# Sampling weights of a deformable convolution: products of mask and hat functions for three offsets in one instruction

## The chip, the core and the metric

The kernel runs on one core of a Trainium2 chip. Its time is the device time of one execution in microseconds (us). The core has five engines that run in parallel, each with its own queue of instructions in a fixed order: TensorE (matrix products; PE in the profile, and PEld for its weight loads), VectorE (DVE), ScalarE (ACT), GpSimd (POOL) and SyncE (SP, which here only starts transfers). An instruction that needs another engine's result, or a buffer that another engine still reads, waits at the head of its queue, and everything behind it waits too.

## The reference, cut to what matters

The kernel computes two layers over four images of 64x64 pixels and 256 channels: a deformable convolution, then an additive attention and a feed-forward layer on half of the tokens. The change lies in the first. There, for every pixel, 8 groups of channels are sampled at 9 points each. A small convolution of the normalised image gives, for each of the 72 points of a pixel, an offset in x, an offset in y and a logit; a softmax over the 9 points of a group makes the logits into masks:

```
offset = x1 @ off_w + off_b
mask = softmax((x1 @ mask_w + mask_b).reshape(N, H, W, G, 9))
out = sum over the points of  mask * bilinear(image, base position + offset)
```

The bilinear sample has four corners whose weights are products of a piecewise linear function (a "hat") of x and one of y.

## The kernel before, in words

The image is not gathered point by point. As long as an offset lies within one pixel, a sample falls on the 3x3 pixels around its base position, and the 9 points of a group together cover a 5x5 window. So the kernel works out, for every pixel and group, 25 weights, the tile `w5` (`w` in the profile), and then sums 25 shifted images times their weights. (Tokens with a larger offset are listed and recomputed by an exact gather of a few rows.)

The first stage is the generator `offsets_and_weights` (lines 267 to 607). It runs over 4 images and, for each, 8 slabs of 512 pixels: 32 turns, each with one "window". Pixels lie on the partitions: a slab is 4 rows of 128. Per turn:

- `taps` (line 492): TensorE makes `po`, the offsets and logits, from the convolution `x1`; VectorE adds the bias into `raw` and begins the softmax. The exponential is ScalarE's (line 513).
- `convolution` (line 462) of the next slab: 9 products per half of the channels on TensorE (`pc`), and a Silu on ScalarE (line 487). For the first image, half of it is made on VectorE (`x<-xn,dwk,x`).
- `window` (line 516): the softmax is finished; ScalarE makes the three hats of every offset, one for each of the pixel offsets -1, 0 and 1, in the tile `hat` [128, 3, 4, 144] (lines 528 to 530 and 533; the first 72 of 144 columns are x, the last 72 y). VectorE clears `w5` (line 537). Then, for each of three row offsets `ey`, `my` is mask times the y hat; for each of three column offsets `ex`, `mxy` is `my` times the x hat, and `mxy` is added to a 3x3 block of `w5` (lines 538 to 547). A product has 4 x 72 = 288 elements per partition.
- `projection` (line 427): TensorE projects the image (`pm`) and transposes it (`ptc`); ScalarE copies it to `tb` (line 456), which goes to memory as the table of the exact gather.
- `turn` (line 550): TensorE transposes `w5` of the turn before (`ptw`), ScalarE copies it, and it is stored to memory (`wt`).
- `front` of the next image: loads of x (`xt`, line 349, a pool `a_ld` with two buffers), transposes `pt`, statistics `st`, `mv`, `gv` on VectorE with two small products `pg` on TensorE, and normalisation.

Beside this stage runs the sampling of image 0 (`sample_image`): VectorE multiplies a shifted image with a loaded weight row (line 827, with `wb` loaded by SP) and adds it up (line 841), 400 instructions of 1024 elements. The main loop at lines 1528 to 1533 takes a fixed number of sampling steps at each `yield` of the stage.

The order on VectorE and on TensorE is that of the program for nearly all of these instructions (`vec` is `pinned`, `pe` is `Pinned`); a scheduler orders ScalarE, and SP's transfers. The stage starts with constants on SP's queue: `inw`, `inb`, `womr` and `wom` (weights of offsets and masks; the offset columns are reordered by VectorE, lines 288 to 292), `ombr`, `omb` (their bias), `dwk` and the normalisation's constants. Their pool `a_one` takes memory that a zero tile `zm` held until its stores to memory are done. What follows the stage (attention, feed-forward, sampling of images 1 to 3) does not use the changed lines.

Of the kernel before, what the change touches and what calls it, by code (L numbers as in the profile page):

```python
# [10 lines left out]
F32 = mybir.dt.float32  # L11
I32 = mybir.dt.int32
AF = mybir.ActivationFunctionType
ALU = mybir.AluOpType
# [3 lines left out]
P = 128  # L18
# [3 lines left out]
CC = C // P  # L22
G, K2 = 8, 9
GP = G * K2
# [22 lines left out]
def layers_kernel(ctx: ExitStack, tc: tile.TileContext, a, out: bass.AP):  # L47
    nc = tc.nc
# [19 lines left out]
    def load_const(pool, name, shape, src):  # L68
        t = pool.tile(shape, F32, name=name)
        nc.sync.dma_start(out=t, in_=src)  # L70
        return t
# [6 lines left out]
    def load_rows(pool, name, src):  # L78

        return load_const(pool, name, [P, src.shape[0]], src.partition_broadcast(P))  # L80
# [74 lines left out]
    with tc.tile_pool(name="selp", bufs=1) as sp, tc.tile_pool(name="ps_c", bufs=2, space=PSUM) as ps_c:  # L155
# [51 lines left out]
        out=below, in_=below, compare_op=ALU.is_gt, fill=0.0, base=0, pattern=[[1, P]], channel_multiplier=-1  # L207
# [27 lines left out]
    S = SimpleNamespace(bank=True, wants=False, gather=True, left=0, tables=[], listing=True)  # L235
# [31 lines left out]
    def offsets_and_weights(images, slab, rows_bufs):  # L267
# [5 lines left out]
        vec, pe = pinned, Pinned(nc.tensor)  # L273
        ca = S.a_one
# [6 lines left out]
        pb = S.a_t.tile([P, CC], F32, tag="pt", name="pb")  # L281
        nc.tensor.matmul(pb, permf, inb.rearrange("p k o -> p (k o)"), start=True, stop=True)
        nc.vector.tensor_copy(inbp, pb)
        womr = ca.tile([P, CC, 2 * GP], F32, name="womr")
        nc.sync.dma_start(out=womr, in_=a["L0_conv_off_w"].rearrange("(k p) f -> p k f", p=P))
        wom = ca.tile([P, CC, 3 * GP], F32, name="wom")
        nc.sync.dma_start(out=wom[:, :, 2 * GP :], in_=a["L0_conv_mask_w"].rearrange("(k p) f -> p k f", p=P))
        for k in range(CC):
# [1 line left out]
                wom[:, k, : 2 * GP].rearrange("p (o s) -> p o s", o=2),  # L290
                womr[:, k].rearrange("p (s o) -> p o s", o=2),
            )
        ombr = load_rows(ca, "ombr", a["L0_conv_off_b"])
        omb = ca.tile([P, 1, 3 * GP], F32, name="omb")
        nc.sync.dma_start(out=omb[:, 0, 2 * GP :], in_=a["L0_conv_mask_b"].partition_broadcast(P))
        nc.vector.tensor_copy(
# [18 lines left out]
        for base, sign in ((0, 1), (7, -1)):  # L315
            nc.gpsimd.affine_select(
                out=gavg, in_=gavg, compare_op=ALU.is_ge, fill=0.0, base=base,
# [101 lines left out]
        def image(at):  # L419
# [96 lines left out]
            def window(s):  # L516
                raw, m3, red, rbc = raws.pop(s)
                vec.tensor_reduce(red, m3, AX.X, ALU.add)
                vec.reciprocal(red, red)
                vec.tensor_tensor(m3, m3, rbc, ALU.mult)  # L520
                nc.sync.dma_start(
                    out=raw_d[n][s * slab * P : (s + 1) * slab * P].rearrange("(t p) j -> p t j", p=P), in_=raw
                )


                off = raw[:, :, : 2 * GP]
                hat = S.a_w1p.tile([P, 3, slab, 2 * GP], F32, tag="hat", name="hat")
                nc.scalar.activation(hat[:, 0], off, AF.Relu, scale=-1.0)
                nc.scalar.activation(hat[:, 2], off, AF.Relu)
                nc.scalar.activation(hat[:, 1], off, AF.Abs)  # L530
                vec.tensor_reduce(omax[:, n, s * slab : (s + 1) * slab], hat[:, 1], AX.X, ALU.max)
                yield
                nc.scalar.activation(hat[:, 1], hat[:, 1], AF.Identity, scale=-1.0, bias=one_c)

                w5 = S.a_wk.tile([P, slab * G, WIN, WIN], F32, tag="w5", name="w5")
                w5s[s] = w5
                vec.memset(w5, 0.0)
                for ey in range(3):
                    my = S.a_w1p.tile([P, slab, GP], F32, tag="my", name="my")
                    vec.tensor_mul(my, raw[:, :, 2 * GP :], hat[:, ey, :, GP:])  # L540
                    for ex in range(3):
                        mxy = S.a_w1p.tile([P, slab, GP], F32, tag="mxy", name="mxy")
                        vec.tensor_mul(mxy, my, hat[:, ex, :, :GP])
                        blk = w5[:, :, ex : ex + 3, ey : ey + 3]
                        vec.tensor_tensor(
                            blk, blk, mxy.rearrange("p t (g i j) -> p (t g) i j", i=3, j=3), ALU.add
                        )
                    yield

            def turn(s):  # L550
# [12 lines left out]

            return SimpleNamespace(
                projection=projection, convolution=convolution, taps=taps, window=window, turn=turn
            )

# [940 lines left out]
    with scope(("one", 1, 0)):  # L1508
        zm = S.one.tile([P, 2 * G * 2 * CG], F32, name="zm")
        nc.gpsimd.memset(zm, 0.0)  # L1510
        for n in range(NB):
            tabw = tab_d[n].rearrange("(q g) c -> q (g c)", g=G)
            for q0 in (0, (H + 2) * MP):
                for f in range(CC):
                    nc.scalar.dma_start(out=xp_d[n][f][:, q0 : q0 + 2 * MP], in_=zm[:, : 2 * MP])
                nc.scalar.dma_start(
                    out=tabw[q0 : q0 + 2 * MP].rearrange("(p r) c -> p (r c)", r=2), in_=zm[:MP]
# [3 lines left out]
    with scope(  # L1521
        ("a_one", 1, 0), ("a_xn", 2, 0), ("a_ld", 2, 0), ("a_wk", 2, 0), ("a_w1p", 1, 0), ("a_sm", 2, 0),
        ("smp", 2, 0), ("two", 2, 0), ("sb", 2, 0), ("dn", 1, 0), ("a_t", 3, 1), ("a_m", 3, 1), ("ps_m", 2, 1),
    ):
        slabs = NT * 2 // SLAB
        S.listing = S.gather = False
        first = sample_image(0, 2)
        for at, i in enumerate(offsets_and_weights(range(NB), SLAB // 2, 1)):
            if i == slabs + 1:
                S.listing = S.gather = True  # L1530

            for _ in range((3, 3, 2, 2, 2)[at % 5] if i < slabs else (4, 4, 3, 3, 3)[at % 5]):
                next(first, None)
        for _ in first:
            pass
# [76 lines left out]
```

## Time and profile before

| | us |
|---|---|
| median of 3 runs | 10418.23 (10410.31 to 10430.02) |
| profiled execution, own time | 10422.25 |
| its span, first to last instruction | 10420.5 |
| first add to `w5` / last add to `w5` (start) | 131.6 / 1341.5 |
| `my` products, 96 of 128x288, mean | 0.458 |
| `mxy` products, 288 of 128x288, mean | 0.458 |
| adds to `w5`, 288 of 128x288, mean | 0.465 |
| TensorE clock granted, mean (1 is full speed) | 0.933 |

The profile is one execution, recorded by the hardware. It has the busy time of each engine, groups of equal instructions with their mean duration, the idle time of the engine just before them, and what ended that idle time. Where a group's idle time is large and the engine is the one that sets the pace, that is where to look; on another engine it costs nothing. Most instructions of this stage carry the line number 263, that of a helper which keeps program order, so that they are told apart by their tiles.

### The profile page before, as it was taken

The page shows a single profiled execution, that of the slowest core. Times are in us where ns is not written, and L with a number is a line of the kernel's source. Part 1 is how long each engine was busy: PE and PEld are TensorE (multiplying, and loading weights), DVE is VectorE, ACT ScalarE, POOL GpSimd, SP SyncE. Part 2 cuts the span into 40 slices and gives each one's busy share as a digit, 9 for nine tenths or more (in the row PEclk, how much of TensorE's full clock was granted, in tenths as well). Part 3 has the DMA queues.
Part 4 walks back from the last instruction along what each step waited for, and adds up shares of the span by engine and source line. Part 5 has one row for each costly group of instructions (what it writes and reads, how often), then busy time and mean ns, then how long its engine had stood idle before and what let it go on. Part 6 is the DMA issues. An engine that isn't in the chain of part 4 may idle for free. (4 is left out here: it accounts for less than half of the span.)

```text
span 10420.5 us, 117367 instructions
## 1 busy us (share of the span) xinstructions
PE 9281.3 (89%) x38892; PEld 4511.9 (43%) x38892; DVE 8523.7 (82%) x13743; ACT 7466.9 (72%) x8526; POOL 5246.2 (50%) x3058
## 2 busy tenths in 40 slices
PE   5777779999999589999999589999999699999995
PEld 3444434444444344444444344444444344444443
DVE  5888879898989579899898679899898367777772
ACT  3333358888888348888888248888887389999991
POOL 0131037775555237676655247676555255555552
PEclk8888879999999689999999689999999799999997
DMA  3565532221222341112111442122111300000002
GB/s 107 179 201 181 179 119 64 64 65 61 72 66 67 129 144 54 51 55 54 53 58 44 144 131 54 53 52 55 53 59 37 103 13 8 10 7 7 7 5 76
DMA packets 375450, 766.10 MB, mean 74 GB/s; under 512 B 49360, under 2 KB 204656, under 8 KB 374800
## 3 DMA queue, kind: packets, MB, share of 16 engines
q1 hardware_dynamic: 282000, 600.32, 17.8%
q0 software_dynamic: 32448, 54.39, 3.2%
q10 hardware_dynamic: 60352, 103.50, 2.8%
q8 instruction: 313, 5.13, 0.2%
q14 instruction: 337, 2.76, 0.1%
HBM read 580.88 MB, written 177.14 MB: 73 GB/s over the span
## 5 line engine op out<-in xcount | busy, mean ns | idle before, releaser
L1035 DVE TENSOR_TENSOR r<-nn,r 128x512 f32<-128x512 f32 x6144 | 3946.0, 684 | 853.7 <-PE nn L1030 793.9
L1030 PE MATMUL nn<-qn,kf 32*128 32x512 f32 (+1 forms) x12288 | 4521.5, 641 | 131.4 <-DVE r L1035 95.2
L1120 POOL TENSOR_TENSOR r<-r 128x1024 f32<-128x1024 f32 x1024 | 2708.6, 2645 | 2656.6 <-DVE r L1035 2613.8
L1114 ACT ACTIVATE r<-d 128x1024 f32<-128x1024 f32 x3072 | 3113.7, 1014 | 1083.5 <-DVE r L1124 705.4
L1020 PE MATMUL d<-qf,kf 32*128 32x512 f32 (+1 forms) x12288 | 3337.6, 632 | 75.3 <-ACT r L1114 74.1
L1116 ACT ACTIVATE r<-r 128x1024 f32<-128x1024 f32 x3072 | 3124.9, 1051 | 32.7
L1030 PEld LDWEIGHTS nn<-qn,kf 32*128 32x128 f32 (+1 forms) x12288 | 1401.4, 185 | 1900.4 <-DVE r L1035 1450.5
L1058 PE MATMUL pv<-v,et 128*128 128x257 f32 x8192 | 2100.0, 399 | 14.5 <-DVE acv L1082 14.5
L1058 PEld LDWEIGHTS pv<-v,et 128*128 128x128 f32 x8192 | 1504.3, 193 | 972.5 <-issue 767.5
L1020 PEld LDWEIGHTS d<-qf,kf 32*128 32x128 f32 (+1 forms) x12288 | 1018.4, 186 | 1339.4 <-issue 690.1
L1122 POOL TENSOR_TENSOR r<-r 128x512 f32<-128x512 f32 x1024 | 1333.4, 1302 | 93.7 <-DVE r L1035 18.0
L827 DVE TENSOR_TENSOR prd<-xs,wb 128x1024 f32<-128x1024 f32 x768 | 979.6, 1275 | 36.1 <-DMA wb<-wt 30.1
L841 DVE TENSOR_TENSOR ac<-ac,prd 128x1024 f32<-128x1024 f32 x768 | 997.3, 1299 | 6.3
L722 POOL DMA_INDIRECT ga<-tab,tii x576 | 698.6, 1213 | 329.4 <-DVE so L736 174.2
L1042 ACT ACTIVATE et<-et,nshift 128x512 f32<-128x512 f32 x1024 | 723.8, 707 | 31.0 <-DVE et L1127 31.0
L1124 DVE TENSOR_TENSOR r<-r 128x512 f32<-128x512 f32 x1024 | 722.8, 706 | 4.1 <-POOL r L1120 3.7
L1127 DVE TENSOR_TENSOR et<-r 128x512 f32<-128x512 f32 x1024 | 699.9, 684 | 0.4
L263 PE MATMUL pc<-xn,diag 128*128 128x512 f32 x1008 | 447.1, 600 | 14.5 <-ACT xn L397 8.3
L263 PE MATMUL ptc<-ident,xp 128*128 128x128 f32 (+1 forms) x576 | 140.3, 359 | 213.9 <-ACT tb L456 212.7
L787 POOL TENSOR_TENSOR xr<-xr,outb 128x512 f32<-128x512 f32 x64 | 90.4, 1419 | 473.6 <-DMA xr<-in_x_dram 416.6
L263 PEld LDWEIGHTS pc<-xn,diag 128*128 128x128 f32 x1008 | 190.9, 192 | 246.1 <-issue 223.0
L1426 POOL DMA_INDIRECT sort<-v,rif x128 | 133.2, 1040 | 291.6 <-DVE rif L263 176.2
(343 smaller groups left out, 5249.2 us busy)
## 6 DMA issues: line engine op xcount, KB each, us to landing
wb<-wt SPq DMA_DIRECT2D x800, 512.0 KB
tab<-tb ACTq DMA_DIRECT2D x128, 256.0 KB
v<-t SPq DMA_DIRECT2D x64, 512.0 KB
xs<-xp SPq DMA_DIRECT2D x32, 680.0 KB
xp<-xp ACTq DMA_DIRECT2D x32, 544.0 KB
xt<-in_x_dram SPq DMA_DIRECT2D x32, 512.0 KB
xr<-in_x_dram SPq DMA_DIRECT2D x64, 256.0 KB
t<-xr SPq DMA_DIRECT2D x64, 256.0 KB
```

The source lines that it names most:

```text
L263: return lambda *args, **kw: keep(op(*args, **kw))
L827: keep(nc.vector.tensor_tensor(pr.rearrange("p (r w) -> p r w", w=W), src, wb.rearrange("p (r w) -> p r w", w=W), ALU.mult,))
L841: keep(nc.vector.tensor_add(ac[:, f, :], ac[:, f, :], pr))
L1020: keep(nc.tensor.matmul(d[:, j, :], kf[g, blk, rows(kt)], qs[q][0][g, blk, :], start=True, stop=True))
L1030: keep(nc.tensor.matmul(nn, kf[g, blk, rows(kt)], qs[q][1][g, blk, :], start=True, stop=True))
L1035: keep(nc.vector.tensor_tensor(r[:, j, :], ns[j], r[:, j, :], ALU.mult))
L1042: keep(nc.scalar.activation(ets[b], ets[b], AF.Exp, bias=nshift))
L1058: keep(nc.tensor.matmul(pv, ets[b0 + i][:, rows(j)], v[:, k0 + i, :], start=(i == 0), stop=(i == PVB - 1)))
L1114: keep(nc.scalar.activation(rs[b, p], ds.pop((b, p)), AF.Ln))
L1116: keep(nc.scalar.activation(rs[b, p], rs[b, p], AF.Exp, scale=-1.0))
L1120: keep(nc.gpsimd.tensor_tensor(rs[b, 1], rs[b, 1], rs[b, 2], ALU.add))
L1122: keep(nc.gpsimd.tensor_tensor(rs[b, 1][:, 0], rs[b, 1][:, 0], rs[b, 3][:, 0], ALU.add))
```

## The change

In `window`, the mask is multiplied with the y hats of all three offsets by one instruction, in place in `hat` (864 elements), and for each `ey` the three x hats are multiplied by one instruction into a tile `mxy` three times as large. The operand that is the same for the three offsets (the mask, or `my` of one `ey`) is read three times, with a stride of zero. The adds to `w5` are as before. A window has 1 + 3 products of 864 elements and 9 adds, where it had 3 + 9 products of 288 and 9 adds.

The larger `mxy` takes memory. To make room, the tiles `womr` and `ombr`, used once at the start, are no longer in the pool of constants: they take the two buffers of the pool `a_ld` that the loads of x (`xt`) use afterwards.

```diff
-        womr = ca.tile([P, CC, 2 * GP], F32, name="womr")
+        womr = S.a_ld.tile([P, CC, 2 * GP], F32, tag="xt", name="womr")
         nc.sync.dma_start(out=womr, in_=a["L0_conv_off_w"].rearrange("(k p) f -> p k f", p=P))
...
-        ombr = load_rows(ca, "ombr", a["L0_conv_off_b"])
+        ombr = S.a_ld.tile([P, 2 * GP], F32, tag="xt", name="ombr")
+        nc.sync.dma_start(out=ombr, in_=a["L0_conv_off_b"].partition_broadcast(P))
...
                 vec.memset(w5, 0.0)
+                mask = raw[:, :, 2 * GP :].rearrange("p t (o k) -> p o t k", o=1).to_broadcast([P, 3, slab, GP])
+                my = hat[:, :, :, GP:]
+                vec.tensor_tensor(my, mask, my, ALU.mult)
                 for ey in range(3):
-                    my = S.a_w1p.tile([P, slab, GP], F32, tag="my", name="my")
-                    vec.tensor_mul(my, raw[:, :, 2 * GP :], hat[:, ey, :, GP:])
+                    mxy = S.a_w1p.tile([P, 3, slab, GP], F32, tag="mxy", name="mxy")
+                    vec.tensor_tensor(
+                        mxy, my[:, ey : ey + 1].to_broadcast([P, 3, slab, GP]), hat[:, :, :, :GP], ALU.mult
+                    )
                     for ex in range(3):
-                        mxy = S.a_w1p.tile([P, slab, GP], F32, tag="mxy", name="mxy")
-                        vec.tensor_mul(mxy, my, hat[:, ex, :, :GP])
                         blk = w5[:, :, ex : ex + 3, ey : ey + 3]
                         vec.tensor_tensor(
-                            blk, blk, mxy.rearrange("p t (g i j) -> p (t g) i j", i=3, j=3), ALU.add
+                            blk, blk, mxy[:, ex].rearrange("p t (g i j) -> p (t g) i j", i=3, j=3), ALU.add
                         )
                     yield
```

## The prediction

> **What bounds the kernel now.** I read the page from the top: engine totals, then the 40 slices, to find what the changed lines overlap with.
>
> ```profile
> PE 9281.3 (89%) x38892; PEld 4511.9 (43%) x38892; DVE 8523.7 (82%) x13743; ACT 7466.9 (72%) x8526; POOL 5246.2 (50%) x3058
> PE   5777779999999589999999589999999699999995
> DVE  5888879898989579899898679899898367777772
> PEclk8888879999999689999999689999999799999997
> ```
>
> A slice is 260.5 us. In the first five TensorE is busy 50 to 70%, VectorE 80%; after that comes attention, with TensorE at 90%. The changed lines run only in the first stage, `offsets_and_weights`, so I asked for the busy time of its later stretches (columns: stretch, length, busy time and count of PE, PEld, DVE, ACT, POOL, then clock, DMA share, GB/s).
>
> ```profile
> 570.00:840.00 270.00, 213.42 (x656) 122.49 (x657) 243.44 (x345) 100.26 (x165) 104.05 (x102) 0.82 0.71 207
> 840.00:1276.00 436.00, 327.53 (x1005) 187.99 (x1004) 388.03 (x537) 150.35 (x248) 34.14 (x26) 0.85 0.57 185
> 1276.00:1345.00 69.00, 51.26 (x172) 33.35 (x172) 30.65 (x64) 24.03 (x43) 3.65 (x4) 0.80 0.29 99
> ```
>
> VectorE is 90% busy from 570 to 1276 us, TensorE 75 to 79%, and from 1276 VectorE only 44%. So VectorE looks like the limit, but not everywhere. What it does there, from the groups of VectorE between 130 and 1345 us (busy, mean ns | idle before, releaser):
>
> ```profile
> L841 DVE TENSOR_TENSOR ac<-ac,prd 128x1024 f32<-128x1024 f32 x192 | 237.5, 1237 | 4.0
> L263 DVE TENSOR_TENSOR w<-w,mxy 128x288 f32<-128x288 f32 x288 | 134.0, 465 | 9.5
> L263 DVE TENSOR_TENSOR mxy<-my,hat 128x288 f32<-128x288 f32 x288 | 131.9, 458 | 12.8 <-ACT hat L533 1.4
> L263 DVE TENSOR_TENSOR my<-raw,hat 128x288 f32<-128x288 f32 x96 | 43.9, 458 | 0.0
> L263 DVE SCALAR_TENSOR_TENSOR x<-xn,dwk,x 128x512 f32<-128x512 f32 x48 | 36.0, 749 | 1.6
> L263 DVE TENSOR_TENSOR raw<-po,omb 128x432 f32<-128x432 f32 x62 | 35.7, 602 | 63.0 <-PE po L263 63.0
> ```
>
> The products to be merged take 131.9 + 43.9 = 175.8 us. The last row is the warning: VectorE waits 63.0 us in this stage for TensorE's `po`. Then what TensorE waits for, same stretch (total, times, longest):
>
> ```profile
> PE ptc L263 <- ACT tb L456: 212.7, 169, 6.4
> PE pmo L783 <- DVE ac L841: 16.5, 4, 12.8
> PE pg L263 <- DVE mv L263: 13.7, 2, 8.9
> PE pg L263 <- DVE gv L263: 10.0, 2, 5.1
> PE pt L263 <- DVE st L263: 9.1, 3, 6.1
> ```
>
> TensorE's large wait is for the copies `tb` on ScalarE, a loop that VectorE has little part in (each `tb` waits for the next `ptc`, or for the store `tab<-tb`). Its waits for VectorE come to some 60 us. So two chains run side by side, of nearly one length: VectorE's, and TensorE with ScalarE.
>
> Last, a window in order of time on VectorE (start, length):
>
> ```profile
> 1255.34 0.72 DVE L263 MEMSET w<- 128x800 f32 x1
> 1255.98 0.40 DVE L263 TENSOR_TENSOR my<-raw,hat 128x288 f32<-128x288 f32 x1
> 1256.41 0.46 DVE L263 TENSOR_TENSOR mxy<-my,hat 128x288 f32<-128x288 f32 x1
> 1256.91 0.46 DVE L263 TENSOR_TENSOR w<-w,mxy 128x288 f32<-128x288 f32 x1
> 1257.47 0.46 DVE L263 TENSOR_TENSOR mxy<-my,hat 128x288 f32<-128x288 f32 x1
> 1257.96 0.46 DVE L263 TENSOR_TENSOR w<-w,mxy 128x288 f32<-128x288 f32 x1
> ```
>
> Dependent instructions start 0.49 us apart. One row offset (my, three mxy, three adds) takes 3.34 us, here from 1255.98 to 1259.32, a window 10.0 us.
>
> **What the Trainium skill says.** "VectorE: DVE Perf Modes", section on the TRN2 errata, gives an fp32 `tensor_tensor` as (N + 151)/0.96 ns and attributes a fixed cost to every instruction. The trace agrees: 457 ns computed for 288 elements against 458 measured, 1224 for 1024 against 1237. "Perfetto Trace Analysis", section Optimization Strategy, says to find the gaps on the engine that limits a regime and what each of them waits for; the 63.0 us above is such a gap, and it shows that VectorE does not limit the whole stage. Neither page prices a broadcast operand in a three-level pattern; the trace shows one, `ga<-ga,wg` 128x1152 at 1352 ns, where the formula gives 1357. So I price the new products, of 864 elements, at (864 + 151)/0.96 = 1057 ns.
>
> **The change, part by part.**
> (1) Products. A window loses 3 + 9 products of 458 ns, 5.50 us, and gains 1 + 3 of 1057 ns, 4.23 us: 1.27 us of busy time. Eight instructions fewer also save eight gaps of about 0.03 us between end and dependent start (0.49 against 0.458): together 1.5 us. 32 windows (4 images, 8 slabs): 48 us of VectorE, if every one counted. The adds into w5 stay, 9 a window.
> (2) All three hats are now needed at the first product, which had needed one. The middle hat (ScalarE, line 533) ended 1.9 us or more ahead of the first product in windows 4 to 27. In 28 it ended 2.8 us after it, of which 1.4 was waited already; in 0 and 2 it ended 0.6 after it. Cost 2.6 us in all, in windows whose gain is lost anyway (below).
> (3) `womr` and `ombr` take the two buffers of `xt`. The first two loads of x, issued at 2.16 us before, now stand on SP's queue behind the constants, the first of which is issued at 61.99 because the zeroing stores hold its memory. With two issues fewer ahead of them they go at about 66.5 and 67.0; a load of x takes some 4 us until its transposes start (the fourth chunk's buffer came free at about 75, its transposes started at 79.04), so the first transposes move from 65.45 to about 70.6. That is covered: the fourth transpose group waited until 74.08 for VectorE's statistics, which wait for `diag`, and `dwk` now arrives two issues (1 us) earlier. Loads 2 to 7 follow one buffer's cycle of 5.9 us and end within 0.5 us of where they did. The megabyte taken from the first microseconds can bring `outw` earlier, for which VectorE idled 1.46 us at 10.37. Taken as zero; ends a gain of 1.5 and a loss of one cycle, 5.9.
> (4) Order. Compiled, every engine has the same instructions after this stage. Within it ScalarE has line 530 ahead of a Silu in some ten windows (0.67 us each way), and the listing of tokens (windows 7 and 8) moves on VectorE and TensorE. VectorE waited 10.3 us for the listing's `pl`; bounds 10 us either way, taken as zero.
>
> **How much arrives.** I keep a lead for each chain. VectorE's grows 1.5 us a window. TensorE's can grow only where it waited for VectorE, by no more than that wait. Where VectorE waited for TensorE, its lead falls back to TensorE's. From the rows in order of time: windows 0 to 4 each run into a wait for `po` (6.2, 1.7, 10.3, 1.8, 4.4 us): lead 0.9 at 282 us, from the 1.2 TensorE waited at 141. 5 to 7 gain, but TensorE, waiting 1.7 through line 533 at 364, takes 1.7 of it: 2.6, and 8 to 10 are lost to waits on `pl` and `po` (3.5 at 517). Window 11, then TensorE waits 8.9 for `mv` at 570: 4.1. 12 lost. 13 and 14, `pmo` waits 2.7 at 663: 6.6. 15 to 17, TensorE waits 1.0 at 757 and 1.9 at 795: 9.5. 18 lost (4.6 at 839). 19 and 20, TensorE waits 1.6 at 916: 11.1. 21 to 23, 0.7 at 1051: 11.8; then VectorE waits 4.4 at 1095 for ScalarE. 25 to 28 stay level, since VectorE waits 0.7, 1.4 and 1.6 for ScalarE there. 29 ends in the 12.8 us wait of `pmo` at 1276: 13.3. 30 lost (7.5 at 1324), and the last window counts whole, as the last `ptw` waited 5.2 us for it: 14.8. So 15 of 48 us. The profiled execution took 10422.25 (span 10420.5 and 1.75 around it): 10407 on its own scale. The median of the runs, 10418.23, lies 4.0 lower: 10403.
>
> **The rivals.**
> Nearly all arrives: VectorE sets the pace throughout, 24 to 48 us, so 10394 to 10370. For: 90% busy against 75 to 79%. Against: the `po` waits, and that TensorE with its `tb` waits is as full.
> Hidden: TensorE and ScalarE set the pace, and their waits for VectorE were slack. Then only the last window counts, less a load cycle: 10423 to 10412. Against: the 12.8 us at 1276.
> Slower: the repeated operand, whose outer stride is zero, does not stream at one element per cycle. At half rate a product takes 1958 ns and a window 2.1 us more; ten windows have waits that absorb it, 22 do not: 46 us, 10464. It decides from 1057 + 1500/4 = 1432 ns on. Against: `ga<-ga,wg`.
> The change does do what it says: the compiled order has 128 products for 384.
>
> **How the numbers follow.** The three runs before span 20 us, so 0.2%, 21 us, is about what can be told from no change. Partial arrival (6 to 21 us) 0.50; nearly all (over 21) 0.28; hidden or a slight loss 0.13; slower by over 21 us 0.09. With a little of the first passing the bound: faster 0.29, same 0.62, slower 0.09. The range goes to 10376 (42 us arrive) and to 10428 (the hidden case with a load cycle lost and the runs' scatter); the likeliest case alone has 10397 to 10412.
>
> **What would show it.** Products of 128x864 at 1.06 us, 128 of them; a window's VectorE work at 8.5 us; waits for `po` longer than 63.0 us in total, as VectorE arrives earlier; the first stage's last w5 add at about 1327 instead of 1341.5; everything later shifted unchanged. Wrong: products over 1.4 us; the last add at 1300; or the first transposes after 75 us.

## The result, and the profile after

The changed kernel took 10401.21 us (median of 11 runs, 10395.03 to 10422.86), the kernel before 10423.14 in the same session (11 runs, 10410.31 to 10434.86): a ratio of 0.9981, with a 95% interval of 0.9972 to 0.9989. That is about 20 us less, 11 to 29. The forecast was 10403, or 15 us less. The profiled execution took 10410.61 us with a span of 10408.9 (before 10422.25 and 10420.5).

The page of the changed kernel, engine totals and two rows of the 40 slices:

```profile
PE 9286.8 (89%) x38892; PEld 4522.6 (43%) x38892; DVE 8493.1 (82%) x13487; ACT 7467.8 (72%) x8526; POOL 5252.1 (50%) x3058
...
PE   5778789999999589999999589999999699999995
...
DVE  6888879898989679899898679899898367777772
```

VectorE has 256 instructions fewer (8 in each of 32 windows) and 30.6 us less of busy time; the slices look nearly as before. The stretches of the first stage (columns as in the prediction: busy time and count of PE, PEld, DVE, ACT, POOL, then clock, DMA share, GB/s):

```profile
570.00:840.00 270.00, 212.38 (x664) 124.27 (x665) 231.75 (x288) 101.65 (x166) 96.90 (x94) 0.82 0.69 201
840.00:1276.00 436.00, 344.87 (x1053) 200.14 (x1052) 369.68 (x445) 151.04 (x248) 35.81 (x28) 0.85 0.56 185
1276.00:1345.00 69.00, 36.38 (x156) 29.53 (x154) 43.94 (x136) 18.48 (x36) 1.85 (x2) 0.62 0.49 170
```

Between 840 and 1276 us VectorE's busy time falls from 388.03 to 369.68 us and TensorE's rises from 327.53 to 344.87: TensorE gets through more of its work in the same time. The last stretch is no longer the same work, since the stage now ends in its middle. VectorE's groups between 130 and 1345 us (busy, mean ns | idle before, releaser):

```profile
L263 DVE TENSOR_TENSOR w<-w,mxy 128x288 f32<-128x288 f32 x288 | 133.3, 463 | 9.3
L263 DVE TENSOR_TENSOR mxy<-hat 128x864 f32<-128x864 f32 x96 | 101.2, 1054 | 1.4
L263 DVE TENSOR_TENSOR raw<-po,omb 128x432 f32<-128x432 f32 x62 | 36.0, 602 | 75.0 <-PE po L263 74.8
...
L263 DVE TENSOR_TENSOR hat<-raw,hat 128x864 f32<-128x864 f32 x32 | 32.5, 1017 | 1.3 <-ACT hat L534 1.1
```

The products take 101.2 + 32.5 = 133.7 us, where they took 175.8. From its first product to its last add, other instructions in between included, a window takes 15.8 us (median of 32), where it took 17.4; the 32 sum to 479.7 us for 526.8. VectorE's wait for `po` has grown from 63.0 to 74.8 us. What TensorE waits for in the same stretch (total, times, longest):

```profile
PE ptc L263 <- ACT tb L457: 199.8, 167, 6.5
PE pmo L787 <- DVE ac L845: 14.6, 3, 10.2
```

These were 212.7 and 16.5. The last window in order of time on VectorE (start, length; x3 is three instructions drawn as one row):

```profile
1301.10 0.72 DVE L263 MEMSET w<- 128x800 f32 x1
1301.92 1.06 DVE L263 TENSOR_TENSOR hat<-raw,hat 128x864 f32<-128x864 f32 x1
1303.01 1.06 DVE L263 TENSOR_TENSOR mxy<-hat 128x864 f32<-128x864 f32 x1
1304.10 1.45 DVE L263 TENSOR_TENSOR w<-w,mxy 128x288 f32<-128x288 f32 x3
1305.58 1.06 DVE L263 TENSOR_TENSOR mxy<-hat 128x864 f32<-128x864 f32 x1
```

The last add into `w5` ends at 1310.7 us, where it ended at 1342.0: 31.3 us earlier. So more was gained in the stage than the 20 us of the whole, and that had to be explained.

### The profile page after: what moved, and what is told of

Its sections match the earlier page's. It is cut to its first block, busy times and chain, and to the rows that moved or that the text cites. A ratio compares the mean times of both kernels' runs of the same rounds, so it can differ in the third digit from the quotient of the medians.

```text
span 10408.9 us, 117078 instructions
## 1 busy us (share of the span) xinstructions
PE 9286.8 (89%) x38892; PEld 4522.6 (43%) x38892; DVE 8493.1 (82%) x13487; ACT 7467.8 (72%) x8526; POOL 5252.1 (50%) x3058
## 5 line engine op out<-in xcount | busy, mean ns | idle before, releaser
L1062 PE MATMUL pv<-v,et 128*128 128x257 f32 x8192 | 2106.5, 401 | 14.8 <-DVE acv L1086 14.8
L1126 POOL TENSOR_TENSOR r<-r 128x512 f32<-128x512 f32 x1024 | 1333.7, 1302 | 100.1 <-DVE r L1039 24.4
```

What stands on the lines that cost most here:

```text
L1062: keep(nc.tensor.matmul(pv, ets[b0 + i][:, rows(j)], v[:, k0 + i, :], start=(i == 0), stop=(i == PVB - 1)))
L1126: keep(nc.gpsimd.tensor_tensor(rs[b, 1][:, 0], rs[b, 1][:, 0], rs[b, 3][:, 0], ALU.add))
```

## The experiments

All kernels ran on the chip beside the kernel before. "Last add" is the end of the last add into `w5` in the profiled execution; "preparation" is the time there between the first and the eighth `mm<-pq,bqk` of VectorE, which are the first and last units of the first attention preparation. The ratio is to the kernel before on the same chip. "Three buffers" is explained with its run.

| kernel | last add, us | preparation, us | ratio, 95% interval |
|---|---|---|---|
| before | 1342.0 | 53.8 | 1 |
| constants moved, products as before | 1332.0 | 62.9 | 1.0003 (0.9994 to 1.0012) |
| changed | 1310.7 | 62.9 | 0.9981 (0.9972 to 0.9989) |
| changed, again | 1317.7 | 56.8 | 0.9975 (0.9963 to 0.9986) |
| changed, matmuls after the stage | 1312.2 | 55.2 | 0.9978 (0.9968 to 0.9988) |
| changed, mxy made twice | 1374.3 | 54.1 | 1.0031 (1.0019 to 1.0042) |
| changed, three adds fewer | 1308.4 | 53.7 | 0.9962 (0.9948 to 0.9977) |
| changed, more copies to tb | 1339.8 | 53.6 | 1.0003 (0.9994 to 1.0012) |
| before, three buffers | 1307.4 | 58.1 | 0.9963 (0.9951 to 0.9976) |
| before, three buffers, again | 1305.6 | 63.0 | 0.9969 (0.9957 to 0.9981) |
| changed, three buffers | 1269.8 | 62.9 | 0.9943 (0.9927 to 0.9960) |
| changed, three buffers, again | 1274.2 | 58.0 | 0.9944 (0.9931 to 0.9957) |
| changed, three buffers, matmuls after the stage | 1282.8 | 63.5 | 0.9951 (0.9937 to 0.9965) |
| changed, three buffers, three adds fewer | 1258.7 | 53.9 | 0.9926 (0.9912 to 0.9940) |

**The changed kernel again.** No edit.

> The changed kernel once more, to see what repeats. Theory A (the clock): the last w5 add again within 3 us of 1310.2, and between 1395 and 1420 us some 9 of the 31 us are given back again, because TensorE stays at half clock until about 1402. Theory B (scatter): the last add or the end of the preparation lies more than 5 us elsewhere, so that the 31 and the 9 say nothing. Time: 10401, ratio 0.998.

Time 10412.75 us against 10442.63 on this chip, ratio 0.9975: the gain is there again, 26 us (15 to 39). But the last add came at 1317.7, 7 us later than in the first profile, and the preparation took 56.8 us, not 62.9. So theory B holds for the details: neither the 31 us nor the giving back of 9 us repeats as it stood. One profile tells the end of this stage to some 7 us (13 us between three executions of one and the same stage with three buffers: 1269.8, 1274.2, 1282.8); the ratios tell more.

**Where the 31 us were gained.** I set the two traces side by side, matmul by matmul, up to the last add. The lead is the start in the kernel before minus the start in the other; each step of it above 0.25 us is put down to the tile at which it appears. Before against changed: `ptc` 10.5, `pmo` 4.7, `ptw` 3.9, `pt` 2.5, `pso` 1.8, `pg` 1.4, the start 2.3, the rest 4.2. The five tiles for which TensorE waited on VectorE (`pmo`, `ptw`, `pt`, `pso`, `pg`) make 14.3 us. Against the second execution of the changed kernel they make 11.4, but there `ptc`, which waits for ScalarE's copies `tb`, makes only 0.9. In its place 9.4 us come at the `po` products, in steps below 0.25 us. These are no waits: the records of `po` start 247 ns apart on average in that execution, for 267 in the kernel before and 263 in the first execution, and fewer of the 512 fall into stretches of half clock (176, for 231 and 220). Between the two executions of the changed kernel, that is with nothing changed at all, `ptc` moves by 8.5 us and `po` by 7.7.

The kernel that has only the constants moved (its run is told below) serves as a second "before": its last add comes at 1332.0. Measured from it, the lead at the last add is 21.3 and 14.3 us; the five tiles make 12.7 and 9.9 of it, `ptc` 8.6 and 0.3. So the part of the five tiles repeats, at 10 to 14 us, and that of `ptc` does not. One place where `ptc` moves is around 1070 us. TensorE there in the kernel before:

```profile
1076.30 0.69 PE L263 MATMUL ptc<-ident,xp 128*128 128x128 f32 x2 [4.67 <-ACT tb L456]
```

The same row in the changed kernel:

```profile
1058.97 0.69 PE L263 MATMUL ptc<-ident,xp 128*128 128x128 f32 x2 [0.86 <-ACT tb L457]
```

And in the kernel that has only the constants moved and makes the products as before:

```profile
1067.01 0.69 PE L263 MATMUL ptc<-ident,xp 128*128 128x128 f32 x2 [0.86 <-ACT tb L457]
```

A wait of 4.67 us becomes one of 0.86 in both, so these 3.8 us are not the products' doing. Behind the 4.67 us ScalarE's copy waits 4.27 us for the store `tab<-tb` that still reads the buffer; in the kernel with only the constants moved the copy at this place waits 0.45 us for it.

**Only the constants moved.** The kernel before, with this part of the diff alone:

```
-        womr = ca.tile([P, CC, 2 * GP], F32, name="womr")
+        womr = S.a_ld.tile([P, CC, 2 * GP], F32, tag="xt", name="womr")
...
-        ombr = load_rows(ca, "ombr", a["L0_conv_off_b"])
+        ombr = S.a_ld.tile([P, 2 * GP], F32, tag="xt", name="ombr")
+        nc.sync.dma_start(out=ombr, in_=a["L0_conv_off_b"].partition_broadcast(P))
```

> The kernel before with womr and ombr moved into the buffers of xt, and nothing else: the products stay twelve. The prediction took this part for nothing: first window at 128.5 to 130.5 for 130.0, last w5 add 1337 to 1345, ratio 0.9995 to 1.0005. Were it part of the gain, the last add would come at 1330 to 1336 and the ratio be near 0.999.

10427.62 us against 10428.63, ratio 1.0003. The first window starts at 129.8 us for 130.0. The last add at 1332.0 would fit the other theory, but the ratio does not: the interval leaves the part a gain of at most 0.06%, of the 0.22% in the whole. Most of the gain, then, is the products', and all of it as far as this run can tell.

**The products made twice.** In the changed kernel:

```
                     mxy = S.a_w1p.tile([P, 3, slab, GP], F32, tag="mxy", name="mxy")
-                    vec.tensor_tensor(
-                        mxy, my[:, ey : ey + 1].to_broadcast([P, 3, slab, GP]), hat[:, :, :, :GP], ALU.mult
-                    )
+                    for _ in range(2):
+                        vec.tensor_tensor(
+                            mxy, my[:, ey : ey + 1].to_broadcast([P, 3, slab, GP]), hat[:, :, :, :GP], ALU.mult
+                        )
```

> Each mxy product is made twice, 1.09 us more each, 3.27 us a window, 105 us of VectorE in 32 windows; the result is the same. If VectorE sets the pace of the stage nearly everywhere, the last w5 add moves from 1310 to 1405-1415 (slope 0.9 to 1). If two chains of one length share it, as the prediction had it (15 of 48), the slope upward still nears 1, since TensorE's chain is then left behind: 1390-1415. If TensorE with ScalarE set the pace and VectorE had slack, below 1370. The whole: plus 60 to 100 us.

59 us more than the changed kernel on the same chip (10471.88 against 10412.75), and a last add 60 us later than the mean of its two profiles (1374.3 against 1314.2): 0.56 of the 105 us. That fits none of the three theories: VectorE does not set the pace nearly everywhere (0.9 to 1), and is not slack (below 1370). Upward too, about half arrives.

**Three adds fewer.**

```
-                    for ex in range(3):
+                    for ex in range(3) if ey != 1 else ():
```

> Leaves out the three adds into w5 of the middle row offset, so the sums lack them: 3 x 0.48 = 1.46 us a window, 47 us of VectorE in 32 windows. If VectorE still sets the pace as it did for the change (31 of 48), the last w5 add comes at about 1280 (slope 0.65). If the TensorE chain is now the limit, as the prediction's leads said, 1295 to 1310 (slope below 0.3), with waits for po far above 75 us.

10398.72 against 10412.75 us: 14 us of 47, with intervals that overlap. (The kernel leaves out three adds in nine, so its weights are incomplete.) The last add, at 1308.4, is 2 to 9 us earlier. VectorE's wait for `po` rises to 89.4 us. This fits the second theory: after the change, VectorE has little left to give.

**More work on ScalarE.** In the changed kernel, each second copy to `tb` is made twice:

```
                         nc.scalar.copy(tb[:m, :, :, c, :], pt[:m, c].rearrange("p f (e g) -> p f g e", g=GH))
+                        if c:
+                            nc.scalar.copy(tb[:m, :, :, c, :], pt[:m, c].rearrange("p f (e g) -> p f g e", g=GH))
```

> The changed kernel with every second copy tb<-ptc made twice on ScalarE: 144 more at 0.39 us, 56 us of ScalarE in the stage, result the same. If the chain of TensorE and ScalarE has no slack after the change, the last w5 add comes 40 to 56 us later, at 1355 to 1370. If its waits are slack behind VectorE, 5 to 20 us later: 1318 to 1335.

The ratio is 1.0003 where the changed kernel has 0.9978 (the mean of 0.9981 and 0.9975): 26 us. The last add moves from 1314.2 to 1339.8, also 26: 0.46 of 56 us. Between the two theories again. VectorE's wait for `po` is now 98.0 us.

**A third buffer for the copies.** In the changed kernel, and the same in the kernel before; `inw` is used up before the first copy, so its 2 KB per partition make the room:

```
-        inw = load_const(ca, "inw", [P, CC, C], a["L0_conv_in_w"].rearrange("(k p) f -> p k f", p=P))
+        inw = S.a_ld.tile([P, CC, C], F32, tag="tb", name="inw", bufs=3)
+        nc.sync.dma_start(out=inw, in_=a["L0_conv_in_w"].rearrange("(k p) f -> p k f", p=P))
...
-                    tb = S.a_ld.tile([P, CC, GH, 2, CG], F32, tag="tb", name="tb")
+                    tb = S.a_ld.tile([P, CC, GH, 2, CG], F32, tag="tb", name="tb", bufs=3)
```

> The changed kernel with a third buffer for tb (inw is loaded into one of them to make room), so that ScalarE's copies wait less for the stores tab<-tb (92 to 99 us in the stage). Theory two chains: after the change TensorE with ScalarE sets the pace, so the stage gains a good part of that: last w5 add at 1285 to 1300, time 10 to 25 us below the changed kernel's. Theory VectorE sets the pace: last add 1308 to 1320, as it was, and ScalarE's wait only moves to another row.

> The kernel before with the same third buffer for tb. If before the change VectorE set the pace, the buffer is worth clearly less here than in the changed kernel: last w5 add 1333 to 1342, ratio 0.9990 to 1.0005. If the two chains wait for each other at many places, it is worth about the same in both: last add 1315 to 1330, ratio 0.998.

The changed kernel takes 10369.19 us, ratio 0.9943; the kernel before 10389.58, ratio 0.9963. ScalarE's wait for the stores, in the changed kernel's stage:

```profile
ACT tb L457 <- DMA tab<-tb: 91.9, 46, 5.9
```

and in the changed kernel with three buffers:

```profile
ACT tb L458 <- DMA tab<-tb: 36.0, 17, 4.2
```

Some 58 us less of waiting (means 95.4 and 37.8 over two profiles each) bring 36 us in the changed kernel and 35 in the kernel before (0.9978 to 0.9943, and 1 to 0.9966). That is more than any theory had expected: the last adds, at 1269.8 and 1307.4, lie ahead of all the ranges. The moved `inw` isn't what brings it, since the first add into `w5` comes at about the same time (133.1 us in the changed kernel for 132.3, 131.3 in the kernel before for 131.6). That it brings about the same in both speaks for the theory of chains that wait for each other at many places, and against the one in which VectorE set the pace before and TensorE after.

**Both again,** to see whether the third buffer lets more of the products' gain arrive:

> The changed kernel with three tb buffers, once more: last w5 add within 8 us of 1269.8, ratio 0.994, the fastest version so far.

> The kernel before with three tb buffers, once more. With the run above it gives what the merged products are worth where no copy waits for a store: if ScalarE's waits for stores were what kept part of the 48 us back, the two last w5 adds lie 33 to 45 us apart (two buffers: 24 to 31). If something else keeps it back, 20 to 31 us.

10366.00 and 10399.21 us, ratios 0.9944 and 0.9969. The last adds lie 31.4 us apart here and 37.6 in the pair above, on either side of the limit of 33 that I had set. The times show no difference: with three buffers the change is worth 0.9944 to 0.9966, 0.0022 or 23 us; with two buffers 0.0022 as well. So nothing shows that the stores keep part of the 48 us back; each ratio is uncertain by 0.0009 to 0.0017, so a difference of 10 us and more could hide. The lead between these traces, taken apart as above in the four pairs of a kernel before and a changed one, has 21 to 25 us at the five tiles and -4.4 to 1.3 at `ptc`. The version with the change and three buffers, 0.9943 and 0.9944, is the fastest that makes the whole computation: about 60 us below the kernel before.

**Three buffers and three adds fewer,** the edit of above:

> The changed kernel with three tb buffers, without the three adds into w5 of the middle row offset (their sums are left out): 47 us less of VectorE. With two buffers this was worth only 2 to 9 us at the last w5 add. If the third buffer gave VectorE the pace, it is now worth 28 to 45 us: last add 1225 to 1245. If TensorE with ScalarE still sets it, under 15 us: 1255 to 1275.

Last add at 1258.7, 13 us before the mean of 1269.8 and 1274.2, and 13 us in the whole. Under 15: the third buffer does not give VectorE the pace.

**Matmuls after the stage.** In the first profile, 9 of the 31 us were gone by the end of the first attention preparation. TensorE's clock was the suspect, so I gave TensorE work ahead of it:

```
+        warm = S.ps_n.tile([P, 512], F32, tag="n", name="warm") if n == 0 else None
+        rw = outwp.rearrange("p k c -> p (k c)")
+        for _ in range(6 if warm is not None else 0):
+            nc.tensor.matmul(warm, ones, rw, start=True, stop=True)
...
+            if warm is not None and i % 4 == 3:
+                nc.tensor.matmul(
+                    warm[:8], mv[:, i - 3 : i + 1, :].rearrange("p i t -> p (i t)"), rw, start=True, stop=True
+                )
```

> The changed kernel plus 14 matmuls of 128x512 whose result nobody reads, between the stage and the first image's attention preparation (6 at once, 8 paced by VectorE's statistics), so that TensorE isn't idle there. If the half clock after a stretch with little work of TensorE gave back the 9 us, the preparation runs at full clock from about 1350, its matmul groups take 2.0 us for 3.8, and it ends 8 to 15 us sooner: about 1410 for 1425, and the lead over the kernel before at 1419 is 28 to 35 us instead of 22. If the clock follows something else, the groups stay at 3.8 us and nothing moves, or 2 to 6 us are lost to the extra matmuls.

10419.04 us, ratio 0.9978 (0.9975 and 0.9981 without them): no gain. The first six depended on nothing and were put at 1298 to 1303 us, inside the stage, so the run tested only half of the idea. With three buffers I tied seven to a tile that is written after the stage:

```
+            nc.gpsimd.memset(kf[:, 0, :512], 0.0)
+            for _ in range(7):
+                nc.tensor.matmul(warm, ones, kf[:, 0, :512], start=True, stop=True)
```

> The changed kernel with three tb buffers, plus 7 matmuls of 128x512 right after the stage, on data that exists only then, and 8 paced by the statistics; nobody reads their result. If TensorE's idle stretch after the stage is what brings the half clock into the first attention preparation, the clock stays full from the stage's end, and the time between the first and the last mm of the preparation falls from 54 to 63 us to 45 to 51. If the half clock comes anyway, it stays at 54 to 63 us, and 0 to 5 us are lost to the extra matmuls.

The preparation took 63.5 us. The whole took 10381.99 us against 10366.00, ratio 0.9951 against 0.9944, with intervals that overlap: nothing is gained. The clock by stretches (columns as above: the clock is the third number from the end):

```profile
1284.40:1302.60 18.20, 13.25 (x28) 4.58 (x27) 8.71 (x45) 2.10 (x3) 0.58 (x2) 0.78 0.97 323
1302.60:1333.00 30.40, 28.80 (x89) 17.63 (x90) 17.81 (x75) 6.88 (x15) 0.97 (x1) 0.50 0.07 20
```

During the added matmuls the clock does become full, for some 10 us in the first of these stretches. Then it is half for 30.4 us, of which TensorE is busy for 28.80; it is full again at the start of the preparation (0.97 from 1334.1 to 1343.5), and half once more (0.51) for 24.0 us. So these matmuls did not keep the clock full. Whether idle time of TensorE brings the half clock is not settled: both stretches of half clock begin in a wait of TensorE (1.21 us for `mv`, 4.92 us for `qe`), and the first seven matmuls multiply zeros, with no run that has other data there. What sets the clock stays open. What it costs can be read. In the kernel before the clock is full from 1399.6 us, 9.3 us into the preparation:

```profile
1390.30:1399.60 9.30, 8.53 (x10) 2.97 (x11) 5.34 (x5) 6.18 (x10) 0.00 (x0) 0.51 0.15 56
1399.60:1444.10 44.50, 42.64 (x124) 17.46 (x122) 39.23 (x36) 12.29 (x12) 3.19 (x2) 1.00 0.57 201
```

In the changed kernel a second stretch of 20.5 us at half clock follows:

```profile
1359.20:1367.80 8.60, 7.81 (x9) 2.70 (x10) 5.36 (x5) 6.13 (x10) 0.00 (x0) 0.51 0.16 61
1371.20:1391.70 20.50, 20.50 (x33) 8.01 (x31) 10.82 (x11) 3.07 (x3) 3.19 (x2) 0.51 0.46 153
1391.70:1422.10 30.40, 29.93 (x85) 12.16 (x84) 26.70 (x26) 8.20 (x9) 0.00 (x0) 1.00 0.50 173
```

and in the kernel with only the constants moved too:

```profile
1393.10:1413.60 20.50, 20.50 (x33) 7.89 (x31) 10.78 (x11) 3.07 (x3) 3.29 (x2) 0.51 0.45 153
```

Both preparations with this stretch take 62.9 us, the one without it 53.8. The kernel with the old products has it, and in the changed kernel's second execution, with 56.8 us, 6.8 us of it are left. TensorE waits 1.11 us for `qe` ahead of the second stretch in the changed kernel, and as long at the same place in the kernel before, where the clock stays full. So the stretch belongs to the execution, not to the change.

## Why the prediction was right, and where it was not

**Products, part (1): right.** 1057 ns was the price; the trace has 1054 ns for `mxy` (1077 in the second execution) and 1017 for the mask's. That is the formula of the Trainium skill, "VectorE: DVE Perf Modes", section on the TRN2 errata, within 4%, and the repeated operand costs nothing on top. Their busy time fell by 42.1 us (39.8 in the second execution; forecast 32 x 1.27 = 40.6). The last window takes 8.8 us from its first product at 1301.92 to the end of its last add at 1310.7; the one before took 10.1. Forecast were 8.5 and 10.0, so this window saves 1.3 us for 1.5. Over all windows the time from first product to last add fell by 47.1 us, for the 48 forecast. With the durations falls the rival of half rate, which needed more than 1432 ns.

**The hats, part (2): right.** The products wait 1.1 us in all for the middle hat; the forecast was 2.6.

**The start, part (3): right.** First transposes at 68.47 us, forecast 70.6 (the constants' first issue came at 59.89 us instead of 61.99), first window at 128.8 for 130.0. The run with that part alone has a ratio of 1.0003.

**Order, part (4): taken as zero, not tested by itself.**

**How much arrives: right in kind, low in size.** The forecast was 14.8 of 48 us at the last add. The two profiles of the changed kernel have 31.3 and 24.4 against the kernel before, and 21.3 and 14.3 against the one with only the constants moved. The whole time is 20 and 26 us less (intervals 11 to 29, which takes in the forecast, and 15 to 39, which begins at it). The weak step is "TensorE's can grow only where it waited for VectorE". At the waits it named, TensorE gained 10 to 14 us in these four pairs, as forecast. What it left out is of two kinds: TensorE's largest wait, 212.7 us for `tb`, where the lead changed by 0.3 to 10.5 us, and TensorE's own speed at the granted clock, where `po` alone brought 0.9 to 9.4. Neither is the same in two executions of one program, so they show as scatter of the size of the excess; whether VectorE's lead has a share in them is not settled. That the first forecast of the whole came within 5 us is partly luck: the second session has it off by 11, and executions of one program differ by as much. The forecast of 1327 for the start of the last add was 10 to 17 us late.

That `tb` is "a loop that VectorE has little part in" isn't shown either. ScalarE makes these copies and the hats in one queue, and for the hats it waits for VectorE, in the stage of the kernel before:

```profile
ACT hat L528 <- DVE raw L263: 110.1, 18, 20.7
```

A copy that stands behind such a wait in ScalarE's queue can be late on VectorE's account. How many are, no run tells.

**"Two chains side by side, of nearly one length": right, and more so than I used it.** 105 us more on VectorE cost 59 (0.56), the change's 48 us less brought 23 (0.48), a further 47 less brought 14 (0.30); 56 us more on ScalarE cost 26 (0.46); 58 us less of waiting for stores brought 36 (0.62). The added and removed times are estimates from counts and durations in the traces, and the intervals of the ratios leave each share uncertain by some 0.2 to 0.4. No engine of this stage sets its time alone. So the rivals "nearly all arrives" and "hidden" are both out.

**"Everything later shifted unchanged": wrong for a single execution.** The lead was 31.3 us at the last add, 22.0 at the end of the preparation and 11.6 at the end. The first step down is the stretch at half clock. The second is no loss of the change either: the kernel with only the constants moved falls back by 10.5 us over the same part (from 0.3 to -10.2), and the changed kernel's second execution as well (from 21.2 to 10.6). It is the one profiled execution of the kernel before that ran this part faster: 8976.4 us, where the other thirteen took 8981.2 to 9000.7.

**Waits for `po` longer than 63.0 us: right**, 74.8 and 72.7.

## What to carry to other kernels

Where two engines of a stage take turns at waiting for each other, a cut in either need not arrive whole: here shares of 0.3 to 0.6 did. A way to learn the share is to add a known amount of work to each and to see how much comes through. Look also at the largest wait that the change does not touch: here a third buffer for copies that wait for their stores was worth more (36 us) than the merged products (23 us), and the two add up. Before a step of a few microseconds in a trace is given a cause, look for it in an execution without the change.

## What the runs showed of the hardware that was not expected

TensorE ran at half clock while it was busy all the time: 20.50 us of 20.50, at a clock of 0.51, in two kernels. The Trainium skill, "TensorE: Matmul & The Clock Gate", Part 1, has the full clock return after one busy window of some 3.4 us; these traces disagree, and the measurement decides. TensorE's ends are modelled in the trace, so this rests on its rows standing without a gap. Fifteen matmuls put ahead of the preparation brought the full clock for some 10 us and did not keep it: 30.4 us at a clock of 0.50 followed, with TensorE busy for 28.80 of them.
